# Two PSUM banks for the sums by bucket, one for the second layer's product, in a graph network's message step

## The chip, the cores and the metric

The kernel runs on one core of a Trainium2 chip. The metric is the device time of one execution in microseconds (us). The core's engines run unsynchronized, each through its own instructions in order: TensorE (PE in the profile, its weight loads PEld), VectorE (DVE), ScalarE (ACT), GpSimd (POOL) and SyncE (SP), which issues most of the DMAs. Matmul results land in PSUM, which has eight banks of 2 KB a partition; the kernel uses all eight in its main part.

## The reference, cut to what matters

There are 12,500 nodes with 64 values each and 212,500 edges, sorted by one of their two ends. With h = relu(layernorm(x)):

```python
edge_in = concatenate([h[row], h[col], dist], axis=1)
e = silu(edge_in @ eW1 + eb1)          # first layer of an edge, 129 -> 128
e = silu(e @ eW2 + eb2)                # second layer, 128 -> 128
agg = segment_sum(e, row, num_segments=12500)
out = x + silu(concatenate([h, agg], axis=1) @ nW1 + nb1) @ nW2 + nb2
```

`row` is not the sorted end, so the sum goes to rows that lie in any order.

## The kernel before, in words

Nodes are dealt to NB = 100 buckets of L = 125. A **sending** part goes through the edges in 208 blocks of 1,024 (lines 376 to 517): it forms an edge's part of the first layer that belongs to its sorted end with a matmul (`qp`, line 463), copies it out of PSUM with ScalarE (`qs`, lines 472 and 473) and scatters its rows with indirect DMAs from GpSimd into a table `q` in DRAM, in which each bucket has places of its own. VectorE finds the place of each edge (`oh`, `each`, `mine`, `rank`, `to`; lines 385 to 439) with the help of two matmuls into the bank `counts` (lines 401 and 420).

A **receiving** part takes those rows back, four buckets and 512 edges at a time. `LEVELS` has 18 levels and there are 25 groups of four buckets, so there are 450 steps. Step k goes through these operations (all four tiles of 128 edges together):

- `s_lr` (571): four PE matmuls write `lr`, the edges' places in their bucket, into a bank of the pool `mm` (four banks, shared with `qp`, `pt` and others).
- `s_one_t` (580): DVE compares `lr` with the node numbers, `oneT` (582), and so frees the bank.
- `s_pt` (585): PE transposes the rows and adds the other end's part through `oneT` (591 and 597) into `pt`; ACT's Silu makes `e1` of it (601) and frees the bank.
- `s_bias` (620): ACT copies the second layer's bias `b2f` into a bank `p2` (623).
- `s_p2` (626): PE adds `e1` times `w2` onto it (629); ACT's second Silu makes `e2` (633).
- `s_one` (604): DVE makes `one` (610); the load of a later step's rows is issued here.
- `s_seg` (636): PE sums `e2` by node into the bank `seg` (643).
- `s_add` (645): DVE adds `seg` to `aggT` (654; for the first level it copies, 652). On the last level this also starts `nodes` (272), the node network for the four buckets.

`manual_schedule` fixes the order on PE, DVE, ACT and SP as the program is written. It is the list `turn` that sets it: turn k issues the operations of several steps, and at each `None` (a hook) some of the sending part's pieces.

```python
        turn = [
            (s_pt, 1), (s_add, -2), (s_one_t, 2), None, (s_bias, 1), (s_p2, 0), (s_one, 0), None, (s_seg, -1), None, (s_lr, 3), None,
        ]
```

The number is how far ahead of k the step is. So in turn k the PE runs `pt` of step k + 1, `p2` of k, `seg` of k - 1 and `lr` of k + 3, with `qp` and `counts` matmuls at the hooks. The PSUM pools are opened at lines 302 to 304:

```python
        mm = work.enter_context(tc.tile_pool(name="mm", bufs=4, space=PSUM))
        p2p = work.enter_context(tc.tile_pool(name="p2", bufs=2, space=PSUM))
        sgp = work.enter_context(tc.tile_pool(name="sg", bufs=1, space=PSUM))
```

The pool `sg` holds one bank for `seg` and one for `counts`. With one bank, `seg` of step k - 1 can't begin before `s_add` of step k - 2 has read the bank. With two banks, `s_bias` of k + 1 writes the bank that the second Silu of step k - 1 has read. The loop at 945 to 948 writes each `p2` bank once with a matmul before the first turn.

Of the kernel before, what the change touches and what calls it, by code (L numbers as in the profile page):

```python
# [28 lines left out]
F32 = mybir.dt.float32  # L29
# [6 lines left out]
PSUM = bass.MemoryType.PSUM  # L36
DRAM = bass.MemoryType.DRAM

P = 128
# [12 lines left out]
G = 4  # L52
# [3 lines left out]
LEVELS = [(1, 18, 0), (1, 32, 0), (1, 46, 0)]  # L56
# [18 lines left out]
def tile_gnn(ctx: ExitStack, tc: tile.TileContext, x, src, dst, ew, eW1, eb1, eW2, eb2, nW1, nb1, nW2, nb2, out):  # L75
    nc = tc.nc
    N, D = x.shape
    H = eW2.shape[0]
    E = src.shape[0]
    assert D == 64 and H == P and N % L == 0  # L80
    NB = N // L
# [81 lines left out]
    b2r = const.tile([1, G, H], F32, name="b2r")  # L163
# [15 lines left out]
    ones = const.tile([1, P], F32, name="ones")  # L179
# [92 lines left out]
    def nodes(B, xr, zh, ps, sb, tag):  # L272

        b = B * G

        zs = sb.tile([P, 2, G // 2, L], F32, name="zs", bufs=3)
        z = [ps.tile([P, G // 2, L], F32, name="z", tag=tag) for _ in range(2)]
        for a in range(2):
            nc.tensor.matmul(z[a], w1g, aggT[:, b + a : b + G : 2, :], start=True, stop=True)
        send_out()  # L280
        yield
        for a in range(2):
            nc.vector.tensor_tensor(zs[:, a], z[a], zh[:, a], op=OP.add)
        nc.scalar.activation(zs, zs, AF.Silu, bias=nb1c)
        yield
        o = ps.tile([L, G, D], F32, name="o", tag=tag)
        for t in range(G):
            nc.tensor.matmul(o[:, t, :], zs[:, t % 2, t // 2, :], w2n, start=True, stop=True)
        yield
        os_ = sb.tile([L, G, D], F32, name="os")  # L290
        nc.vector.tensor_tensor(os_, o, xr, op=OP.add)
        unsent.append((out_rows[:, b : b + G, :], os_))
# [7 lines left out]
    top = ctx.enter_context(tc.tile_pool(name="to", bufs=4))  # L300
    with ExitStack() as work:
        mm = work.enter_context(tc.tile_pool(name="mm", bufs=4, space=PSUM))
        p2p = work.enter_context(tc.tile_pool(name="p2", bufs=2, space=PSUM))
        sgp = work.enter_context(tc.tile_pool(name="sg", bufs=1, space=PSUM))
        work.enter_context(
            tc.manual_schedule(
                engines={mybir.EngineType.PE, mybir.EngineType.DVE, mybir.EngineType.Activation, mybir.EngineType.SP}
            )
        )
        full = sgp.tile([P, NB], F32, name="counts")  # L310
        nc.tensor.matmul(full, before, identb[:, :NB], start=True, stop=True)
        nc.vector.memset(full, -1.0)
        mine = cnt.tile(twos, F32, name="mine")
# [209 lines left out]
        steps = [(w, B, n, g) for w, B, n in batches for g in range(n)]  # L523
# [118 lines left out]
            for t, (j, b) in enumerate(tiles):  # L642
                nc.tensor.matmul(item[2][:, b, :], e2[:, t, :], one[:, t, :], start=j < G, stop=j >= G * (n - 1))  # L643

        def s_add(k):
            c, B, n, g = steps[k]
            if g < n - 1:
                return
            v = aggT[:, B * G : B * G + G, :]
            seg = batch.pop((c, B))[2]  # L650
            if c == 0:
                nc.vector.tensor_copy(v, seg)
            else:
                nc.vector.tensor_tensor(v, v, seg, op=OP.add)  # L654
            if c == len(LEVELS) - 1:
                tails.append(nodes(B, *node_in.pop(B), mm, ndp[1], "mm"))
# [2 lines left out]


        turn = [
            (s_pt, 1), (s_add, -2), (s_one_t, 2), None, (s_bias, 1), (s_p2, 0), (s_one, 0), None, (s_seg, -1), None, (s_lr, 3), None,
        ]
        hooks = sum(1 for s in turn if s is None)
        def norm(xs, n, early=False):

            xs = xs[:, :n, :]
            wide = [P, n, D]
            mean = fp.tile([P, NE], F32, name="mean")[:, :n]
            nc.vector.tensor_reduce(mean, xs, AX.X, OP.add)  # L670
            nc.vector.tensor_scalar(mean, mean, 1.0 / D, None, op0=OP.mult)
            cen = fp1.tile([P, NE, D], F32, name="cen")[:, :n]
            nc.vector.tensor_tensor(cen, xs, mean[:, :, None].to_broadcast(wide), op=OP.subtract)
            if early:
                nc.vector.tensor_tensor(xs, cen, cen, op=OP.mult)
            else:
                nc.scalar.activation(xs, cen, AF.Square)
            yield
            var = fp.tile([P, NE], F32, name="var")[:, :n]
            nc.vector.tensor_reduce(var, xs, AX.X, OP.add)  # L680
            nc.vector.tensor_scalar(var, var, 1.0 / D, EPS, op0=OP.mult, op1=OP.add)
            nc.scalar.activation(var, var, AF.Sqrt)
            yield
            nc.vector.reciprocal(var, var)
            nc.vector.scalar_tensor_tensor(xs, cen, 0.0, var[:, :, None].to_broadcast(wide), op0=OP.max, op1=OP.mult)
            yield
# [27 lines left out]
        def normed(b0, n, xs):  # L714
            yield from norm(xs, n)
            yield
            ready.add(b0)
# [158 lines left out]
        with tc.tile_pool(name="lists", bufs=1, side="right") as lp:  # L876
# [23 lines left out]
            nc.sync.dma_start(x0[:, G:, :], x0_rows[:, G:, :])  # L900
            extra_rows(nc.sync.dma_start)
            near, far = norm(x0[:, :G, :], G, True), norm(x0[:, G:, :], NE - G)
            places, table = destinations(), first_rows(0)
            next(near)
# [37 lines left out]
        aggp = ctx.enter_context(tc.tile_pool(name="aggp", bufs=1))  # L942
        aggT = aggp.tile([P, NB, L], F32, name="aggT")
        b2f = aggp.tile([P, G, H], F32, name="b2f")
        for _ in range(2):
            p2 = p2p.tile([P, G, H], F32, name="p2")
            nc.tensor.matmul(p2, ones, b2r, start=True, stop=True)
            nc.scalar.copy(b2f, p2)
        ld2 = work.enter_context(tc.tile_pool(name="ld2", bufs=NQ))
        ndp, lap = [], []  # L950
        pieces = send_all(2 * FIRST, nblocks)
# [13 lines left out]
        for w in range(1, len(LEVELS)):  # L965
            start = w * (NB // G) - NQ
# [2 lines left out]
            marks.append((hooks * (by - first), goal_of(w)))  # L969
        at = 0  # L970
        for k in range(first, len(steps) + 2):
            for s in turn:
                if s is None:
                    while len(marks) > 1 and at >= marks[1][0]:
                        marks.pop(0)
                    if len(marks) > 1:
                        (t0, n0), (t1, n1) = marks[:2]
                        goal = n0 + (n1 - n0) * (at + 1 - t0) / (t1 - t0)
                        while done + 1 <= goal + 0.001:
                            next(pieces, None)  # L980
                            done += 1
                    at += 1
                    for _ in range(2):
                        if not lap and next(feed, 0) == 0:
                            feeding.close()
                            lap.append(keeping.enter_context(tc.tile_pool(name="la", bufs=1, side="right")))
                    if tails:
                        both = tails[at % 2 :: 2][:1] if len(tails) > 1 else tails[:1] * (at % 2)
                        for t in both:
                            if next(t, 0) == 0:  # L990
                                tails.remove(t)
                else:
                    f, ahead = s
                    if 0 <= k + ahead < len(steps):
                        f(k + ahead)
            if k == len(steps) - 8:
                assert done == total
                fp = mm.tile([1, P], F32, name="fp", tag="mm")
                s = cnt.tile([P, 1], F32, name="s")
                nc.vector.tensor_tensor(s, bad[:, 0:1], bad[:, 1:2], op=OP.add)  # L1000
                nc.tensor.transpose(fp, s, ident)
                m = cnt.tile([1, 1], F32, name="m")
                nc.vector.tensor_reduce(m, fp, AX.X, OP.max)
                nc.vector.tensor_copy(flag_i, m)
# [137 lines left out]
```

## Time and profile before

| | |
|---|---|
| median of three runs | 2978.04 us (2963.86 to 2979.62) |
| the profiled execution | 2986.03 us |
| its span, first to last instruction | 2984.2 us |
| sending alone, and the tables | from 0 to about 330 us |
| sending and receiving together | from about 330 to about 2740 us |
| receiving alone, and the node network | from about 2740 us to the end |
| mean granted TensorE clock | 0.877 |

A row of the timeline has the start and the length in us, the engine, the line and the operation, and in brackets how long the engine had been idle and what released it. A row of the waits has the total in us, the number of waits and the longest. A PE row gives the time at which a matmul was taken up; several rows are merged into one with a count.

### The profile page before, as it was taken

To read this page: it belongs to the slowest core of one execution; us is meant where nothing else is said; L and a number is where in the kernel's file an instruction comes from. 1 tells how busy PE (TensorE), PEld (TensorE's weight loads), DVE (VectorE), ACT (ScalarE), POOL (GpSimd) and SP (SyncE) were. 2 spreads that over 40 slices of the span, in tenths; PEclk is the share of its full clock that TensorE was granted. 3 is DMA by queue.
4 is the path that set the end of the run, shared out by engine and by line. 5 is a ranking of instruction groups with operands and counts; after the bars stand their busy time and mean duration, and the time that the engine had idled before them with its cause. 6 is when DMAs were issued, how large, how long until landed. Compare 5 with 4: busy or idle time off the path is not lost.

```text
span 2984.2 us, 49759 instructions
## 1 busy us (share of the span) xinstructions
PE 2368.6 (79%) x17391; PEld 2043.5 (68%) x17391; DVE 1882.5 (63%) x3250; ACT 1165.9 (39%) x3258; POOL 1700.0 (57%) x1712
## 2 busy tenths in 40 slices
PE   2664677778888888888788877888787888888998
PEld 1442566667777777766677766777676777777998
DVE  7553455566666666666666666666666666666755
ACT  2432333334344444433344333344333434344543
POOL 5665656666565655655665566565655656565410
PEclk8555788889998999989899889988988998899999
DMA  4443555444444444444444344443443333333374
GB/s 104 165 156 125 188 181 161 142 141 131 140 139 132 137 136 138 134 128 128 131 140 136 121 131 133 135 135 122 143 143 120 104 106 101 106 104 109 115 225 133
DMA packets 244993, 402.91 MB, mean 135 GB/s; under 512 B 49516, under 2 KB 143647, under 8 KB 244529
## 3 DMA queue, kind: packets, MB, share of 16 engines
q1 hardware_dynamic: 151717, 217.57, 24.7%
q0 software_dynamic: 53536, 123.03, 11.9%
q10 hardware_dynamic: 39482, 59.04, 7.0%
q8 instruction: 139, 2.28, 0.3%
q14 instruction: 119, 0.97, 0.1%
HBM read 192.46 MB, written 207.01 MB: 134 GB/s over the span
## 4 chain that ended last, share of the span: by engine, by line
PE 62%; another core or an unknown queue 15%; issue 8%; ACT 6%; DVE 5%; DMA 2%; SPq 0%; POOL 0%; ACTq 0%; DVEq 0%; POOLq 0%
PE pt L597 13%; PE p L629 12%; PE seg L643 11%; PE qp L463 9%; PE pt L591 7%; PE lr L577 4%; ACT e L601 2%; PE ab L206 2%; DMA qt<-q 1%; ACT qs L472 1%; DVE aggT L654 1%; DVE oneT L582 1%; ACT p L623 1%; PE counts L401 1%
## 5 line engine op out<-in xcount | busy, mean ns | idle before, releaser
L476 POOL DMA_INDIRECT q<-qs,to x1661 | 1669.3, 1005 | 1142.1 <-issue 424.1
L601 ACT ACTIVATE e<-pt 128x512 f32<-128x512 f32 x450 | 269.4, 599 | 1181.4 <-remote 440.7
L654 DVE TENSOR_TENSOR aggT<-aggT,seg 128x500 f32<-128x500 f32 x425 | 285.4, 672 | 496.1 <-remote 133.4
L643 PE MATMUL seg<-one,e 128*128 128x125 f32 x3600 | 528.0, 290 | 79.4 <-DVE aggT L654 46.3
L629 PE MATMUL p<-w,e 128*128 128x128 f32 x3600 | 540.1, 296 | 18.4 <-issue 18.3
L643 PEld LDWEIGHTS seg<-one,e 128*128 128x128 f32 x3600 | 466.6, 201 | 115.8 <-issue 58.6
L629 PEld LDWEIGHTS p<-w,e 128*128 128x128 f32 x3600 | 493.2, 210 | 41.8 <-issue 36.5
L463 PE MATMUL qp<-win,pick 64*128 64x256 f32 x1662 | 386.5, 469 | 110.9 <-ACT e L601 40.2
L582 DVE TENSOR_SCALAR oneT<-lr,part 125x512 f32<-125x512 f32 x450 | 336.0, 747 | 155.4 <-remote 40.0
L472 ACT COPY qs<-qp 128x256 f32<-128x256 f32 x831 | 310.9, 375 | 285.8 <-PE p L629 67.3
L591 PE MATMUL pt<-ident,qt 128*128 128x128 f32 x1800 | 315.7, 303 | 92.3 <-ACT e L601 54.9
L435 DVE TENSOR_TENSOR mine<-oh,counts 128x800 f32<-128x800 bf16 x208 | 204.4, 982 | 221.9 <-PE qp L463 65.3
L633 ACT ACTIVATE e<-p 128x512 f32<-128x512 f32 x450 | 270.0, 600 | 166.4 <-PE p L629 49.2
L463 PEld LDWEIGHTS qp<-win,pick 64*128 64x128 f32 x1662 | 173.5, 205 | 215.0 <-issue 76.4
L577 PE MATMUL lr<-identb,qt 128*125 128x128 bf16 x1800 | 196.7, 231 | 140.7 <-ACT e L601 63.2
L591 PEld LDWEIGHTS pt<-ident,qt 128*128 128x128 f32 x1800 | 213.8, 155 | 133.1 <-ACT e L601 64.3
L610 DVE TENSOR_TENSOR one<-nodes,qt 128x500 f32<-128x500 f32 x450 | 303.4, 674 | 0.0
L597 PE MATMUL pt<-oneT,al 125*128 125x128 f32 x1944 | 300.9, 305 | 3.1 <-issue 2.9
L577 PEld LDWEIGHTS <-qt 128*125 128x125 bf16 x1800 | 167.2, 144 | 178.5 <-issue 149.2
L597 PEld LDWEIGHTS pt<-oneT,al 125*128 125x128 f32 x1944 | 279.1, 220 | 3.6 <-issue 3.5
L623 ACT COPY p<-b2f 128x512 f32<-128x512 f32 x450 | 269.0, 598 | 0.0
L437 DVE TENSOR_REDUCE rank<-mine 128x8 f32<-128x800 f32 x208 | 205.1, 986 | 7.2
(156 smaller groups left out, 1907.5 us busy)
## 6 DMA issues: line engine op xcount, KB each, us to landing
qt<-q SPq DMA_DIRECT2D x450, 288.0 KB
q<-zeros ACTq DMA_DIRECT2D x70, 720.0 KB
q<-qs,to POOLq DMA_INDIRECT x1661
bc<-dests SPq DMA_DIRECT2D x103, 128.0 KB
win<-tb SPq DMA_DIRECT2D x416, 30.0 KB
tb<-got SPq DMA_DIRECT2D x25, 256.0 KB
a_last<-ta SPq DMA_DIRECT2D x25, 256.0 KB
zd<-zn SPq DMA_DIRECT2D x25, 250.0 KB
```

Of the source, the lines that this page charges most:

```text
L463: nc.tensor.matmul(qps[i_][:, :m], pick[half, t * P : (t + 1) * P], win[half, :m], start=True, stop=True)
L472: nc.scalar.copy(qs[:, :m, :H], qp[:, :m, :])
L476: ins = nc.gpsimd.indirect_dma_start(out=q[:], out_offset=bass.IndirectOffsetOnAxis(ap=to[:k, j : j + 1], axis=0), in_=qs[:k, a, :], in_of ...
L577: nc.tensor.matmul(lr[:L, t, :], loc[:, at : at + 1].to_broadcast([P, L]), identb, start=True, stop=True)
L582: nc.vector.tensor_scalar(oneT, st[k].pop("lr")[:L], part1[:L, :], None, op0=OP.is_equal)
L591: nc.tensor.matmul(pt[:, t, :], qt[:, j, :H], ident, is_transpose=True, start=t == 0, stop=False, skip_group_check=True)
L597: nc.tensor.matmul(pt[:, cols, :], a[:L, b, :], oneT[:, cols, :], start=False, stop=True, skip_group_check=True)
L601: nc.scalar.activation(e1, pt, AF.Silu)
L610: nc.vector.tensor_tensor(one.rearrange("p (b j) l -> p b j l", j=n), nodes1[:, None, None, :].to_broadcast(wide), loc[:, tiles[0][1] : ti ...
L629: nc.tensor.matmul(p2[:, t, :], e1[:, t, :], w2, start=False, stop=t == G - 1, skip_group_check=True)
L643: nc.tensor.matmul(item[2][:, b, :], e2[:, t, :], one[:, t, :], start=j < G, stop=j >= G * (n - 1))
L654: nc.vector.tensor_tensor(v, v, seg, op=OP.add)
```

## The change: what it does

- `sg` gets two banks, so `seg` of one step and of the next lie in different ones. `counts` gets a pool of its own, with one bank. `p2` gets one bank instead of two. The sum is eight, as before.
- `s_add` moves from its place after `s_pt` to a place ahead of `s_seg`, for all levels but the last. On the last level it stays where it was.
- `s_bias` of step k + 1 moves from ahead of `s_p2` of step k to behind it, so ACT copies the bias after the second Silu of the step before, into the bank which that Silu has read.
- In the last two turns `s_seg` comes first.
- The loop that writes the `p2` banks once becomes a single pass.

```diff
-        p2p = work.enter_context(tc.tile_pool(name="p2", bufs=2, space=PSUM))
-        sgp = work.enter_context(tc.tile_pool(name="sg", bufs=1, space=PSUM))
+        p2p = work.enter_context(tc.tile_pool(name="p2", bufs=1, space=PSUM))
+        cp = work.enter_context(tc.tile_pool(name="cp", bufs=1, space=PSUM))
+        sgp = work.enter_context(tc.tile_pool(name="sg", bufs=2, space=PSUM))
...
-        full = sgp.tile([P, NB], F32, name="counts")
+        full = cp.tile([P, NB], F32, name="counts")
...
-        def s_add(k):
+        def s_add(k, late=False):
             c, B, n, g = steps[k]
-            if g < n - 1:
+            if g < n - 1 or late != (c < len(LEVELS) - 1):
                 return
...
-            (s_pt, 1), (s_add, -2), (s_one_t, 2), None, (s_bias, 1), (s_p2, 0), (s_one, 0), None, (s_seg, -1), None, (s_lr, 3), None,
+            (s_pt, 1), (s_add, -2), (s_one_t, 2), None, (s_p2, 0), (s_bias, 1), (s_one, 0), None,
+            (lambda k: s_add(k, True), -2), (s_seg, -1), None, (s_lr, 3), None,
         ]
         hooks = sum(1 for s in turn if s is None)
+        ending = [(s_seg, -1)] + [s for s in turn if s is None or s[0] is not s_seg]
...
-        for _ in range(2):
-            p2 = p2p.tile([P, G, H], F32, name="p2")
-            nc.tensor.matmul(p2, ones, b2r, start=True, stop=True)
-            nc.scalar.copy(b2f, p2)
+        p2 = p2p.tile([P, G, H], F32, name="p2")
+        nc.tensor.matmul(p2, ones, b2r, start=True, stop=True)
+        nc.scalar.copy(b2f, p2)
...
-            for s in turn:
+            for s in turn if k < len(steps) else ending:
```

In the built programs the order of the instructions on PE, SP and POOL is the same before and after, but for the matmul of the dropped pass and the last `seg`; only DVE and ACT have another order.

## The prediction

> **What bounds the kernel now.** I read the page first, its busy times, slices and chain:
>
> ```profile
> PE 2368.6 (79%) x17391; PEld 2043.5 (68%) x17391; DVE 1882.5 (63%) x3250; ACT 1165.9 (39%) x3258; POOL 1700.0 (57%) x1712
> ...
> PE   2664677778888888888788877888787888888998
> ...
> PEclk8555788889998999989899889988988998899999
> ...
> PE 62%; another core or an unknown queue 15%; issue 8%; ACT 6%; DVE 5%; DMA 2%; SPq 0%; POOL 0%; ACTq 0%; DVEq 0%; POOLq 0%
> PE pt L597 13%; PE p L629 12%; PE seg L643 11%; PE qp L463 9%; PE pt L591 7%; PE lr L577 4%; ACT e L601 2%; PE ab L206 2%; DMA qt<-q 1%; ACT qs L472 1%; DVE aggT L654 1%; DVE oneT L582 1%; ACT p L623 1%; PE counts L401 1%
> ```
>
> PE is the busiest engine and holds most of the chain; ACT, at 39%, has room. Then the stretches, since sending and receiving overlap only until about 2740 us:
>
> ```profile
> 330.00:2740.00 2410.00, 1974.46 (x14570) 1711.64 (x14569) 1552.25 (x2644) 947.35 (x2666) 1439.49 (x1438) 0.90 0.43 132
> 2740.00:2984.00 244.00, 230.83 (x2022) 222.21 (x2020) 151.44 (x274) 110.28 (x227) 65.39 (x70) 0.98 0.52 155
> ```
>
> The columns are the length, then PE, PEld, DVE, ACT, POOL, the clock and the DMA. After 2740 PE is busy 230.83 of 244 us: little to win. Before, PE idles 2410 - 1974 = 436 us. So the change is decided in that stretch. Its waits, PE's alone (total us, times, longest), and from the view of line 643 those for the addition with weight loads included:
>
> ```profile
> PE lr L577 <- ACT e L601: 63.2, 36, 4.6
> PE pt L591 <- ACT e L601: 54.9, 31, 3.9
> PE seg L643 <- DVE aggT L654: 46.3, 49, 2.6
> ...
> PE qp L463 <- ACT e L601: 40.2, 25, 3.7
> ...
> PE pt L591 <- ACT qs L472: 21.8, 27, 2.7
> ...
> PE lr L577 <- ACT qs L472: 9.2, 7, 2.4
> ...
> PE qp L463 <- ACT qs L472: 8.1, 10, 2.0
> ...
> PE qp L463 <- DVE oneT L582: 5.4, 5, 3.1
> PE lr L577 <- DVE oneT L582: 4.5, 12, 0.8
> ```
>
> ```profile
>   DVE aggT L654: 88.6, 86
> ```
>
> The change goes at the third row: 46.3 us seen by the matmuls, 88.6 us with the loads, which partly see the same wait. The rows on `e` (63.2 + 54.9 + 40.2 = 158 us) are waits for a bank of `mm` and stay.
>
> **One such wait in full.** The timeline, PE, then DVE, then ACT:
>
> ```profile
> 1514.28 0.36 PE L629 MATMUL p<-w,e 128*128 128x128 f32 x1 [0.45 <-issue]
> 1516.45 1.16 PE L643 MATMUL seg<-one,e 128*128 128x125 f32 x8 [1.80 <-DVE aggT L654]
> 1517.45 0.39 PE L577 MATMUL lr<-identb,qt 128*125 128x128 bf16 x4
> ...
> 1518.46 0.62 PE L591 MATMUL pt<-ident,qt 128*128 128x128 f32 x4
> ```
>
> ```profile
> 1515.72 0.68 DVE L654 TENSOR_TENSOR aggT<-aggT,seg 128x500 f32<-128x500 f32 x1 [2.08 <-PE p L629]
> 1516.32 0.74 DVE L582 TENSOR_SCALAR oneT<-lr,part 125x512 f32<-125x512 f32 x1
> ```
>
> ```profile
> 1516.21 0.60 ACT L601 ACTIVATE e<-pt 128x512 f32<-128x512 f32 x1
> 1516.70 0.60 ACT L623 COPY p<-b2f 128x512 f32<-128x512 f32 x1
> 1517.21 0.60 ACT L633 ACTIVATE e<-p 128x512 f32<-128x512 f32 x1
> 1517.70 0.38 ACT L472 COPY qs<-qp 128x256 f32<-128x256 f32 x1
> ```
>
> ACT and DVE both stand still until about 1515.7 and then run off at once what they owe: PE's results reach them in a bunch. These bunches set the rhythm of the stretch; the change doesn't remove them. It changes only how far PE may run ahead until the next bunch, and what it waits for behind it.
>
> **The change part by part.** The sum is made against the profiled execution, 2986.03 us; the runs shown have their median at 2978.04, 8.0 lower, so I take 8.0 off at the end.
>
> *Two banks for `seg`, and the later addition.* `seg` then needs the addition of two steps before, long done. In the example it could go at 1514.64 instead of 1516.45, 1.81 us sooner. What is late next: `lr`, at 1517.45, wants its bank from `oneT`, which stands behind the addition. With that gone from ahead of it `oneT` ends about 0.6 sooner, at 1516.46, so `lr` gains about 0.9. Next `pt`, at 1518.46, wants a bank that the `qs` copy of 1517.70 (ends 1518.08) frees, and gains only 0.3. So of a wait between a sixth and a half is kept: of 88.6 us 15 to 44; the ends are nothing kept and all of it. I take 0.4, nearer the half because several of the waits have `lr`, not `pt`, next: **-35 us** (0 to -88.6).
>
> *`oneT` ahead of the addition.* PE's rows on `oneT`: 5.4 in 5 waits and 4.5 in 12. At most an addition's 0.68 goes from each: 5 x 0.68 + 4.5 = 7.9. I take **-7** (0 to -9.9). VectorE's own time is the same. The late addition waits for a `seg` of the turn before, so it holds up nothing that stands behind it (the hooks' `mine`, `rank` and `to`, on which POOL waits).
>
> *One bank for `p2`.* Now `p2` of step k + 1 waits for the bias copy, that for the second Silu of k, and that for `p2` of k. Before, the copy was done ahead of the Silu. A Silu and a copy take 0.60 + 0.60, with about 0.05 to hand over, so `p2` may start 1.25 us after the Silu's start. Where ACT was late anyway (1516.70, 1517.21) Silu and copy only change places. Where ACT waited for `p2` itself it bites; in the trace of before 18 turns have a Silu that waited and a next `p2` less than 1.25 us behind its start, the first and the last of them being
>
> ```profile
> 529.16 0.60 ACT L633 ACTIVATE e<-p 128x512 f32<-128x512 f32 x1 [1.54 <-PE pt L591]
> ```
>
> ```profile
> 529.84 2.09 PE L629 MATMUL p<-w,e 128*128 128x128 f32 x8
> ```
>
> ```profile
> 2618.92 0.60 ACT L633 ACTIVATE e<-p 128x512 f32<-128x512 f32 x1 [2.19 <-PE pt L597]
> ```
>
> ```profile
> 2618.36 0.39 PE L629 MATMUL p<-w,e 128*128 128x128 f32 x2
> ...
> 2620.33 0.38 PE L629 MATMUL p<-w,e 128*128 128x128 f32 x2 [0.82 <-issue]
> 2622.61 1.13 PE L643 MATMUL seg<-one,e 128*128 128x125 f32 x8 [1.90 <-DVE aggT L654]
> ```
>
> The first lacks 529.16 + 1.25 - 529.84 = 0.57 us, the last 2618.92 + 1.25 - 2618.36 = 1.81; the 18 together 26.3. The last also shows why not all of it is lost: `p2` would start at 2620.17, take 0.9, and `seg` could follow at 2621.1, still ahead of its 2622.61, as it no longer waits for the addition. I take half, **+13 us** (0 to 26.3).
>
> *The bias copy behind the Silu.* ACT's total is the same, but where the Silu had to wait, the copy filled that wait before; now it stands ahead of what follows, mostly the `qs` copies, which free banks for PE and feed POOL. The group of the second Silu in the stretch, and its idle time:
>
> ```profile
> L633 ACT ACTIVATE e<-p 128x512 f32<-128x512 f32 x397 | 238.4, 601 | 147.4 <-PE p L629 30.6 <-remote 26.7 <-PE qp L463 21.3
> ```
>
> It idles 147.4 us ahead of the 397. The copy also has to wait for the Silu's end, where before the Silu began 0.51 us after a copy of 0.60 (1516.70, 1517.21): some 0.1 us a turn, in ACT's spare time. PE waited for `qs` 27 + 7 + 10 = 44 times; were each of them 0.65 later, it would be 29 us. Only those behind a Silu that waited are, I take a third: **+9 us** (0 to 29).
>
> *The rest.* The dropped pass of `p2` lies at 140 us, ahead of any turn; its two matmul passes are 2 x 1.06 us. In that slice of 75 us, the second in the page, PE is busy six tenths, so the idle rest covers it and I cost it at nothing; at -2 if not covered:
>
> ```profile
> L947 PE MATMUL p<-b2r,ones x4: 1056/1056/1215, 140.0 to 142.7; 1*128 1x512 f32 x4
> ```
>
> The last turns gain at most one `seg`, under 1.2 us: nothing. No DMA moves, and SP's and POOL's orders stay.
>
> The sum: -35 - 7 + 13 + 9 = -20 us. 2986.03 - 20 = 2966; less 8.0 that is **2958 us** as a median, 0.7% below 2978.04.
>
> **A rule of the Trainium skill.** "TensorE: Matmul & The Clock Gate", section "HAM oscillation — how this bites in real kernels", says of one kernel that "Adding PSUM double-buffering gave no further gain". That speaks against the first term; by it the gain would be 0, and it bears on the third rival. Here the row of 46.3 us shows a real wait for the bank, but also three times as much for other banks, so the trace neither refutes nor confirms it.
>
> **The rivals.**
>
> - *The second layer's bank takes the wait over (slower).* The one-bank loop isn't gone, it moves from `seg` to `p2`: a bunch that comes late now stops PE one product sooner, and its way back is longer: Silu and copy, 1.25 us, instead of an addition, 0.68 + 0.05. If all 49 of PE's waits come back so, nothing is won, 49 x (1.25 - 0.73) = 25 us are lost, and the two ACT terms make it more: 25 + 9 = 34, less 7 for `oneT`: 2978 + 27 = **3005 us**. It decides from the point where PE is less than 1.25 us behind the Silu's start in more than about 49 turns; in the trace of before it is 18, which speaks against it. For it speaks that PE will run further ahead there.
> - *All of the wait goes, and ACT's terms stay hidden.* 46.3 + 9.9 = 56 us: 2978 - 56 = **2922 us**. Against it: `lr` and `pt` in the example.
> - *The next bank takes it over (no change).* `e`'s 158 us are bank waits of `mm` at `lr`, `pt` and `qp`, PE's next instructions. If they grow by what `seg` loses, -35 becomes about -15 (the sixth) and the sum is -15 - 7 + 13 + 9 = 0: **2978 us**.
> - *It doesn't do what it says.* `seg` still waits for DVE, for `one`; were DVE late with the addition by a whole turn, the wait would stay. DVE, busy 1552 of 2410 us, is not: this belongs to the no-change case.
>
> **How the numbers follow.** The forecast has 0.36, all of it gone 0.12, no change 0.27, taken over by `p2` 0.25. What a measurement of this kernel can tell from no change is about 0.5%, 15 us. The forecast lies 20 us below with neighbours on both sides of that line; a sliver of 0.02 of it I give to the no-change side, and as much of no change to faster. So faster 0.48, same 0.27, slower 0.25. The range: from 2915, where the matmuls' 46.3 and the loads' part of `oneT` go and ACT costs nothing (2978 - 56, and 7 for a third of a hundredth more clock: 1974 x 0.0033 / 0.90), to 3005, the slower rival. Cases of both signs are likely, so beside it the forecast's own range, from its first term alone (44 to 15 us): 2949 to 2978.
>
> **What would show it.** In the stretch to 2740: `seg`'s wait for `aggT` should be nearly gone (under 5 us from 46.3), the step that I am surest of. PE's waits for `e` should grow by 10 to 25 us. A new row, PE `p` waiting for ACT `p`, should stand at 10 to 20 us; at 40 or more the slower rival is right. PE's waits for `qs` should go from 39 to about 48. PE's idle time in the stretch should fall by some 20 us, and the stretch after 2740 stay within 2 us. Wrong would I be if the bunches themselves change, since everything else is measured against them, or if the clock leaves 0.90.

## The result, and the profile after

The changed kernel is slower: 2998.43 us as a median of 16 runs (2984.72 to 3013.08), against 2970.32 for the kernel before in 16 runs (2955.02 to 2985.0). The ratio is 1.0093, with a 95% interval of 1.0078 to 1.0109. The forecast was 2958: 20 us to the good, where 28 were lost. The profiled execution took 3004.4 us (span 3002.6), at a mean clock of 0.876.

The page of the changed kernel: busy times, slices of PE and its clock, and the chain. Line numbers are one higher than before.

```profile
PE 2377.1 (79%) x17389; PEld 2052.5 (68%) x17389; DVE 1874.2 (62%) x3250; ACT 1228.1 (41%) x3257; POOL 1701.2 (57%) x1712
...
PE   2664776778888888888778887888777888888998
...
PEclk9655788888898899988988989899888888899999
...
PE 62%; another core or an unknown queue 13%; issue 9%; ACT 7%; DVE 5%; DMA 2%; POOL 0%; SPq 0%; ACTq 0%; DVEq 0%; POOLq 0%
PE p L630 13%; PE pt L598 13%; PE seg L644 11%; PE qp L464 8%; PE pt L592 8%; PE lr L578 4%; ACT e L634 2%; ACT e L602 2%; PE ab L206 2%; ACT qs L473 2%; DMA qt<-q 1%; DVE oneT L583 1%; PE counts L402 1%; PE z L279 1%
```

The addition (`aggT`) and the bias copy (`p`) are no longer among the chain's lines; the second Silu (`e` L634) has come in, and `qs` has gone from 1% to 2%. ACT is busy 62 us longer, though it does one instruction less. The stretches, with the columns as before:

```profile
330.00:2740.00 2410.00, 1960.96 (x14456) 1703.83 (x14452) 1529.62 (x2622) 993.38 (x2647) 1430.03 (x1429) 0.89 0.43 131
2740.00:2984.00 244.00, 235.19 (x2059) 226.69 (x2057) 157.73 (x283) 123.39 (x239) 76.29 (x80) 0.98 0.53 160
```

In the same 2410 us PE takes up 14,456 matmuls instead of 14,570, 0.8% fewer: the loss lies in the sending and receiving stretch. PE idles 2410 - 1961 = 449 us there, from 436. PE's waits in that stretch:

```profile
PE pt L592 <- ACT e L602: 56.2, 37, 4.2
PE pt L592 <- ACT qs L473: 55.4, 35, 3.8
PE lr L578 <- ACT e L602: 49.0, 25, 4.3
...
PE qp L464 <- ACT e L602: 43.9, 21, 6.4
...
PE qp L464 <- DVE oneT L583: 20.9, 13, 5.2
PE qp L464 <- ACT qs L473: 18.2, 15, 3.2
...
PE p L630 <- ACT p L624: 11.6, 15, 1.8
...
PE p L630 <- ACT e L634: 8.3, 5, 2.8
```

There is no row for `seg` waiting on `aggT` any more; it was 46.3 us. In its place the rows on `qs`, with one more of 2.8 us at `lr`, make 76.4 us, from 39.1, and `p2` waits 19.9 us for ACT where it waited for no engine. The waits for `e` didn't grow: 149.1 from 158.3. On ACT, the second Silu in that stretch:

```profile
L634 ACT ACTIVATE e<-p 128x512 f32<-128x512 f32 x394 | 236.0, 599 | 265.7 <-PE p L630 84.1 <-remote 47.5 <-PE pt L598 29.3
```

ACT idles 265.7 us ahead of it instead of 147.4. What filled that time before, the bias copy, now runs behind the Silu.

The loss can be read from GpSimd too. Its scatters in the page of before and in that of the changed kernel:

```profile
L476 POOL DMA_INDIRECT q<-qs,to x1661 | 1669.3, 1005 | 1142.1 <-issue 424.1
```

```profile
L477 POOL DMA_INDIRECT q<-qs,to x1661 | 1669.8, 1005 | 1159.3 <-issue 424.9
```

They take as long as before, and GpSimd idles 17.2 us longer ahead of them, where the span has grown by 18.4. In the stretch its waits for `qs` go from 533.4 to 555.5 us. The last scatter ends at 2829 us before and 2846 after, so sending doesn't end at 2740 as the table ahead of the prediction has it; and in all twenty traces of this case the program ends 156 to 158 us after its last scatter. What is lost or gained shows in when that one comes.

### The profile page after: what moved, and what is told of

Read it like the earlier page. It is cut to its first block, busy times and chain, and to the rows that moved or that the text cites. A ratio compares the mean times of both kernels' runs of the same rounds, so it can differ in the third digit from the quotient of the medians.

```text
span 3002.6 us, 50305 instructions
## 1 busy us (share of the span) xinstructions
PE 2377.1 (79%) x17389; PEld 2052.5 (68%) x17389; DVE 1874.2 (62%) x3250; ACT 1228.1 (41%) x3257; POOL 1701.2 (57%) x1712
## 4 chain that ended last, share of the span: by engine, by line
PE 62%; another core or an unknown queue 13%; issue 9%; ACT 7%; DVE 5%; DMA 2%; POOL 0%; SPq 0%; ACTq 0%; DVEq 0%; POOLq 0%
PE p L630 13%; PE pt L598 13%; PE seg L644 11%; PE qp L464 8%; PE pt L592 8%; PE lr L578 4%; ACT e L634 2%; ACT e L602 2%; PE ab L206 2%; ACT qs L473 2%; DMA qt<-q 1%; DVE oneT L583 1%; PE counts L402 1%; PE z L279 1%
## 5 line engine op out<-in xcount | busy, mean ns | idle before, releaser
L630 PE MATMUL p<-w,e 128*128 128x128 f32 x3600 | 552.1, 302 | 24.7 <-ACT p L624 11.6
L630 PEld LDWEIGHTS p<-w,e 128*128 128x128 f32 x3600 | 502.0, 215 | 52.9 <-issue 20.9
L644 PEld LDWEIGHTS seg<-one,e 128*128 128x128 f32 x3600 | 473.2, 203 | 53.2 <-issue 45.7
L634 ACT ACTIVATE e<-p 128x512 f32<-128x512 f32 x450 | 269.4, 599 | 310.6 <-PE p L630 122.4
L598 PE MATMUL pt<-oneT,al 125*128 125x128 f32 x1944 | 292.1, 299 | 2.3 <-issue 2.3
L598 PEld LDWEIGHTS pt<-oneT,al 125*128 125x128 f32 x1944 | 270.1, 214 | 2.3 <-issue 2.2
L624 ACT COPY p<-b2f 128x512 f32<-128x512 f32 x450 | 265.4, 590 | 14.1
L598 PE MATMUL pt<-oneT,ae 125*128 125x128 f32 x1360 | 212.4, 303 | 9.5 <-issue 9.0
```

The costliest lines, as they stand in the source:

```text
L598: nc.tensor.matmul(pt[:, cols, :], a[:L, b, :], oneT[:, cols, :], start=False, stop=True, skip_group_check=True)
L630: nc.tensor.matmul(p2[:, t, :], e1[:, t, :], w2, start=False, stop=t == G - 1, skip_group_check=True)
L634: nc.scalar.activation(e2, p2, AF.Silu)
```

## The experiments

**Theories.** *A:* ScalarE's order costs the time. The bias copy now stands between the second Silu and the `qs` copies, which free PE's banks and feed GpSimd. *B:* the single `p2` bank costs it: PE's product must wait for the Silu and the copy. *C:* the later addition holds VectorE up.

**Two kinds of batches.** Each batch ran the kernel before beside its own kernels, on one chip. In three of the five batches before took 2399, 2399 and 2404 us, at a mean granted clock of 0.948 to 0.949; in two it took 2925 and 2969 us, like the 2970 of the result, at 0.883 and 0.879. So there are two sets of results, which I call the 2400 and the 2950 runs. That the chip makes the difference isn't shown: the record gives the same chip number for one of the batches at 2399 us and for the one at 2969. Times are compared only within a batch, ratios only within a set.

GpSimd differs as well. Its row in the changed kernel's page in a 2400 run (experiment 5):

```profile
L477 POOL DMA_INDIRECT q<-qs,to x1661 | 1676.4, 1009 | 538.0 <-issue 305.5
```

It idles 538 us ahead of its scatters instead of 1159. From 330 us on, 5 of its pauses are longer than 0.35 us, 8 us in all, against 310 pauses and 672 us in the changed kernel's trace at 3003 us. So in the 2400 runs GpSimd goes from one scatter to the next with little more than a steady 0.3 us between them, and what PE and ACT wait for has little room to cost or save time.

All ratios, with their 95% intervals:

| kernel | 2950 runs | 2400 runs |
|---|---|---|
| the changed kernel | 1.0093 [1.0078, 1.0109], 1.0074 [1.0045, 1.0102], 1.0118 [1.0085, 1.0152] | 0.9963 [0.9950, 0.9976] |
| before, copy behind the Silu | 1.0053 [1.0028, 1.0079] | 1.0019 [1.0005, 1.0034] |
| the same, one `p2` bank | 1.0093 [1.0062, 1.0123] | 1.0015 [1.0004, 1.0026] |
| changed, early addition | not measured | 1.0004 [0.9994, 1.0014], 1.0013 [0.9999, 1.0027] |
| changed, copy at the end of the turn | 1.0016 [0.9989, 1.0042] | 0.9964 [0.9952, 0.9975] |
| changed, copy in the middle | 0.9981 [0.9956, 1.0006] | 0.9973 [0.9959, 0.9987] |
| before, copy in the middle | not measured | 1.0002 [0.9990, 1.0015] |
| before, no copy | 0.9943 [0.9921, 0.9965] | 1.0001 [0.9986, 1.0015] |
| changed, no copy | 0.9938 [0.9914, 0.9962] | 0.9982 [0.9967, 0.9997] |

Where I give the difference of two medians of one batch, the interval in brackets is from resampling their runs.

**1. The bias copy behind the Silu, nothing else.** In before's `turn`:

```diff
-None, (s_bias, 1), (s_p2, 0), (s_one, 0), None,
+None, (s_p2, 0), (s_bias, 1), (s_one, 0), None,
```

> The kernel before with one edit: the bias copy stands behind the second Silu; two p2 banks and one seg bank stay, and the addition stays early. Theory A (ScalarE's order: the copy now stands ahead of the qs copies, which free banks for the PE): 15 to 35 us slower than before, and the PE's waits for the qs copies between 330 and 2740 us rise from 39.1 to 65 us or more. Theory B (the single p2 bank makes the PE wait for Silu and copy): within 6 us of before, since with two banks the bank that the copy takes has long been read; qs waits at 39 to 45. Theory C (the late addition holds VectorE up): within 6 us of before.

> Before, with only the bias copy of the next step put behind the second Silu; two p2 banks, one seg bank, early addition. On a chip that takes 2970 us theory A (the copy stands ahead of the qs copies) asks for 15 to 30 us more than before and for PE's waits on qs to go from 39 to over 65 us; theory B for no difference over 5 us, since p2 keeps two banks; the seg wait on aggT stays at 40 us or more in both. On a chip that takes 2400 us the earlier look gave 1.0019, and it should come again within 0.002.

In the 2400 run it costs 4 us (2403.43 against 2399.35). In the 2950 run it costs 15.7 us [9, 22], within A's 15 to 30. But PE's waits on `qs` are at 43.1 us there, not over 65 (before wasn't traced in that batch), and a new one is nearly as large, though `p2` still has two banks:

```profile
PE pt L591 <- ACT qs L472: 31.4, 27, 4.4
PE p L629 <- ACT p L623: 31.0, 19, 3.1
```

So the order alone makes the product wait: the copy for the next step can't begin before a Silu that itself waits for PE. B expected no difference from this kernel; A expected another row. `seg` waits 33.9 us for `aggT`, where 40 or more was expected.

**2. The same, and `p2` with one bank.**

```diff
-        p2p = work.enter_context(tc.tile_pool(name="p2", bufs=2, space=PSUM))
+        p2p = work.enter_context(tc.tile_pool(name="p2", bufs=1, space=PSUM))
```

> The kernel before with the copy behind the Silu and one p2 bank; one seg bank, and the addition early. Theory A: within 8 us of the run with two banks and the copy behind, so 15 to 35 us slower than before. Theory B: 30 to 60 us slower than before (the changed kernel's 28 us and what two seg banks give back), with the PE waiting 20 us or more for the bias copy or the second Silu. Theory C: within 6 us of before.

> The same as the run with the copy behind the Silu, and p2 with one bank. Its difference to that run is the price of the single bank alone. Theory B: 10 us or more on a chip that takes 2970 us, with a wait of p2 on the copy and the Silu of 15 us or more in PE; theory A: under 5 us, the loss being there already with two banks. On a chip that takes 2400 us the earlier look had 1.0015 against 1.0019: nothing.

In the 2950 run the loss of the second `p2` bank costs 18.4 us [4, 24] more; in the 2400 run nothing (-1.5 [-6, 4]). B asked for 10 us or more, and has it; A asked for under 5. But B's reason doesn't show: `p2` waits 16.0 + 11.9 = 27.9 us, less than the 31.0 with two banks, while the waits on `qs` go from 43.1 to 68.3. What the bank does to ACT shows in the timeline. With two banks (the kernel of experiment 1), ACT:

```profile
1002.72 0.60 ACT L633 ACTIVATE e<-p 128x512 f32<-128x512 f32 x1 [0.36 <-PE p L629]
1003.22 0.59 ACT L623 COPY p<-b2f 128x512 f32<-128x512 f32 x1
1003.73 0.38 ACT L472 COPY qs<-qp 128x256 f32<-128x256 f32 x1
```

With one bank (the changed kernel), ACT, and then PE:

```profile
1529.89 0.60 ACT L634 ACTIVATE e<-p 128x512 f32<-128x512 f32 x1 [0.97 <-PE lr L578]
1530.52 0.59 ACT L624 COPY p<-b2f 128x512 f32<-128x512 f32 x1
1531.04 0.37 ACT L473 COPY qs<-qp 128x256 f32<-128x256 f32 x1
```

```profile
1529.24 0.70 PE L464 MATMUL qp<-win,pick 64*128 64x256 f32 x4
1531.46 0.66 PE L592 MATMUL pt<-ident,qt 128*128 128x128 f32 x4 [1.51 <-ACT e L634]
```

With two banks the copy begins 0.50 us after the Silu's start, ahead of its end; with one it begins 0.63 after it, behind its end, since it writes the bank that the Silu reads (0.49 and 0.63 us are the medians of the 449 such pairs in each of the two traces). So `qs` begins 1.15 us after the Silu's start instead of 1.01; in the copy's own place it could begin at 0.50. In the last fence PE takes up `pt` at 1531.46, 0.05 us after the `qs` copy's end at 1531.41. (The row names the Silu, but that had ended at 1530.49.) With the copy out of the way that could be 0.65 us sooner.

**3. The changed kernel with the addition at its early place.**

```diff
-            if g < n - 1 or late != (c < len(LEVELS) - 1):
+            if g < n - 1 or late:
```

> The changed kernel with the addition early on every level, as before. Theories A and B: within 6 us of the changed kernel, so 22 to 34 us slower than before. Theory C: 10 to 25 us faster than the changed kernel, and the PE's waits for oneT fall from 29.5 us between 330 and 2740 us to about 10.

> The changed kernel with the addition back at its early place on all levels. Against the changed kernel (1.0074 on a chip where before takes 2925 us, 1.0093 where it takes 2970 us) it is the price of the move alone. Theory C (the late addition holds VectorE up): 5 us or more faster than the changed kernel, 1.003 to 1.006, and PE's waits on oneT fall. My own forecast: slower than the changed kernel by 3 to 8 us, 1.009 to 1.011, since oneT stands behind the addition again. On a chip that takes 2400 us it gave 1.0004 before.

Both batches were 2400 ones: 1.0004 and 1.0013, where the changed kernel has 0.9963. The early addition is the slower place there, by some 10 us, the other way round from C. For the 2950 runs, where the loss is, it stays untried; but experiments 7 and 8 keep the later addition and lose nothing there, so C can't be the main cause.

**4. The changed kernel with the copy at the end of the turn,** behind the `qs` copies of all the turn's hooks:

```diff
-(s_p2, 0), (s_bias, 1), (s_one, 0), None,
+(s_p2, 0), (s_one, 0), None,
...
-(s_seg, -1), None, (s_lr, 3), None,
+(s_seg, -1), None, (s_lr, 3), None, (s_bias, 1),
```

> The changed kernel with the bias copy at the end of a turn, behind the last hook, where ScalarE next waits for pt. One p2 bank, two seg banks and the late addition stay. Theory A: 20 to 40 us faster than the changed kernel, so from 12 us faster than before to 8 slower; the PE's waits for the qs copies fall from 76 us to 35 to 50. Theory B: no faster than the changed kernel, as the copy comes later still and p2 waits for it at least as long (20 us or more). Theory C: within 6 us of the changed kernel.

> The changed kernel with the bias copy put at the very end of the turn, behind the qs copies of all hooks. Theory A: on a chip that takes 2970 us the loss of 28 us goes, PE's waits on qs fall from 76 to under 50 us and the time is at or below before's (0.985 to 1.002). Theory B: p2 waits longer still, as the copy comes later, over 40 us, and the time is 1.01 or more. On a chip that takes 2400 us 0.996 should come again within 0.002.

In the 2950 run it takes 17.7 us [12, 26] from the changed kernel's loss. PE's waits in it:

```profile
PE p L630 <- ACT p L624: 75.9, 49, 4.3
...
PE pt L592 <- ACT qs L473: 24.2, 19, 3.0
```

The waits on `qs` are 31.0 us in all, from 58.0 in the changed kernel of the same batch. `p2` waits for the copy 75.9 us, from 30.7, and the kernel is still faster. This is against B as the main cause, and says that a long row of PE's waits needn't cost its length.

For A speaks that in this batch the waits on `qs` stand in the order of the times. PE's and GpSimd's up to 2740 us are 31 and 486 us here (2932.54 us as a median), 43 and 509 in experiment 1 (2940.60), 58 and 524 in the changed kernel (2950.18), 68 and 543 in experiment 2 (2958.97). It is one trace of each.

**5. The changed kernel again,** without an edit, in three batches.

> The changed kernel itself, unedited, beside the kernel before on whatever chip this falls on. The kernel before took 2970 us on the chip of the result and 2399 us on the chip of the first experiments. If the loss comes from the edits themselves (theories A, ScalarE's copy ahead of the qs copies, and B, PE waiting for Silu and copy in the one p2 bank), the ratio is above 1.004 on either chip. If it needs the late bunches of the chip that takes 2970 us, it is 1.008 to 1.011 there and within 0.3% of 1 on a chip that takes 2400 us. The early addition gave 1.0004 on the quick chip; theory C (the late addition holds VectorE up) asks for more than 1.002 here on such a chip.

> The changed kernel itself. Where before takes 2925 to 2970 us: 1.006 to 1.010, as measured twice. Where before takes 2400 us it hasn't been timed: its relatives there gave 1.0004 and 1.0013 with the addition early, 0.9964 with the copy at the end of the turn and 0.9973 in the middle, so if the copy's place matters there too, 0.999 to 1.002; if only the early addition had cost something, 0.996.

> The changed kernel itself again. Where before takes 2925 to 2970 us: 1.007 to 1.012, as measured three times. Where before takes 2400 us, for the first time: 0.996 to 0.999, since the copy in the middle gave 0.9973, at the end of the turn 0.9964, and PE hardly waits for ScalarE there, so the copy's place should matter little; 1.000 or more would say that it matters there too.

In the 2950 runs it loses 25 and 34 us. In the 2400 run it gains 7.9 us [6, 14]: 2395.91 against 2403.83. The same program is slower on the one and faster on the other. So the edits alone don't decide the sign.

**6. Before without the bias copies,** so that the output lacks the second layer's bias:

```diff
-            nc.scalar.copy(p2, b2f)
...
-                    p2[:, t, :], e1[:, t, :], w2, start=False, stop=t == G - 1, skip_group_check=True
+                    p2[:, t, :], e1[:, t, :], w2, start=True, stop=True, skip_group_check=True
```

> Before, with the copies of the second layer's bias left out (the product starts the bank itself), so the output lacks that bias; banks and places as in before. 450 copies of 0.60 us go from ScalarE, which before did in its idle time or ahead of the second Silu. Theory A (what counts is what stands ahead of the qs copies on ScalarE): a gain of 15 us or more, with PE's waits on qs below 25 us from 39. Theory B (what counts is how long one turn of Silu and copy holds p2, and ScalarE's load doesn't matter): within 10 us of before, 0.997 to 1.003.

> Before, without the copies of the second layer's bias, so the output lacks that bias. Where before takes 2925 to 2970 us, theory A (what counts is what stands ahead of the qs copies on ScalarE) asks for a gain of 15 us or more and PE's waits on qs below 25 us; theory B (the loop through p2 counts, ScalarE's load doesn't) for 0.997 to 1.003. Where before takes 2400 us: 1.000 again, within 0.0015.

**7. The changed kernel without them,** by the same edit.

> The changed kernel without the bias copies, so the output lacks that bias too. p2 has one bank and must still wait for the second Silu of the step before, but not for a copy. Theory A: the loss goes with the copy, and the two seg banks show their gain; the time is below that of the run without the copy and with before's banks by some 10 us (two copies of the same chain, 0.3%). Theory B: the one bank alone still costs; p2's waits on the Silu stay above 20 us and the time is above that of the run without the copy and with before's banks.

> The changed kernel without the bias copies (the output lacks that bias): one p2 bank, two seg banks, late addition. Where before takes 2925 to 2970 us, theory A: 0.990 to 0.997, below the run without the copies on before's banks, since the loss went with the copy. Theory B: 1.002 or more, with waits of p2 on the second Silu of 20 us or more, since the one bank still makes the product wait. Where before takes 2400 us: 0.998 again, within 0.0015.

In the 2400 runs the copies are worth nothing to before (2399.09 against 2399.16). In the 2950 runs before gains 16.5 us [9, 27] without them and the changed kernel 51.5 us [42, 63]: 2952.24 and 2950.80 us are left, -1.4 us [-9, 4] apart. So all of the loss hangs on the copy, and one `p2` bank without a copy costs no more than two `seg` banks with the later addition bring. B in its plain form falls: it asked for 20 us of waits of `p2` on the Silu, and there are 8.0. A has the gain that it asked for, but not its row: PE still waits 35.6 us for `qs` in before without the copies, not under 25. The stretch to 2740 us in before without the copies, PE's waits and the stretch itself:

```profile
PE lr L577 <- ACT e L601: 64.3, 31, 5.5
PE pt L591 <- ACT e L601: 61.6, 39, 4.0
PE seg L642 <- DVE aggT L653: 60.9, 49, 3.4
PE qp L463 <- ACT e L601: 36.5, 21, 6.1
...
PE seg L642 <- issue: 21.1, 39, 2.3
```

```profile
330.00:2740.00 2410.00, 1995.82 (x14841) 1737.19 (x14841) 1573.99 (x2680) 771.10 (x2300) 1459.22 (x1454) 0.90 0.45 133
```

And in the changed kernel without them:

```profile
PE pt L592 <- ACT e L602: 75.0, 42, 4.8
PE qp L464 <- ACT e L602: 44.1, 24, 5.3
PE seg L643 <- issue: 42.0, 75, 1.2
...
PE lr L578 <- ACT e L602: 36.5, 23, 4.6
...
PE counts L421 <- DVE counts L419: 17.6, 8, 4.2
```

```profile
330.00:2740.00 2410.00, 2007.47 (x14886) 1744.74 (x14883) 1565.54 (x2683) 772.79 (x2305) 1460.28 (x1456) 0.90 0.45 134
```

60.9 us of waiting for `aggT` are gone, and the matmuls done are 45 more of 14,841, 0.3%. Most of the wait has moved, as PE's idle time in the stretch falls by only 11.7 us: for `e` it is 162.4 and 155.6, with `pt` taking what `lr` had; `counts` waits 17.6 instead of 8.1, and `seg` 42.0 instead of 21.1 with nothing shown to wait for.

**8. The changed kernel with the copy in the middle of the turn,** behind the second hook, so behind the `qs` copies that come right after the Silu:

```diff
-(s_p2, 0), (s_bias, 1), (s_one, 0), None,
+(s_p2, 0), (s_one, 0), None, (s_bias, 1),
```

> The changed kernel with the copy behind the second hook, so behind that hook's qs copies and ahead of the later ones: a place between the changed kernel's (1.0074 on a chip where before takes 2925 us) and that at the end of the turn (1.0016). Theory A: between the two, 1.002 to 1.006, with PE's waits on qs between 31 and 58 us. Theory B: p2's waits between 40 us (changed) and 78 us (end of the turn), and the time above the changed kernel's, since the copy comes later for the product.

> The changed kernel with the copy behind the second hook. Where before takes 2925 to 2970 us: theory A, between the changed kernel and the one with the copy at the end of the turn, 1.002 to 1.006; theory B, above the changed kernel, 1.008 or more. Where before takes 2400 us: 0.9973 again, within 0.0015.

In the 2950 run it is 37.4 us [26, 52] faster than the changed kernel: all of the loss is gone, more than A's graded forecast of 1.002 to 1.006, and the opposite of B's. PE waits for `qs` 40.1 us, from 61.1 in the changed kernel of that batch, and for the copy not much longer (19.9 from 14.1). PE's waits on `qs` stand in the order of the times in this batch too: 32, 36, 40 and 61 us for 2951 and 2952 (experiments 7 and 6), 2965 and 3002; GpSimd's, 516, 518, 515 and 537, only set the last apart. In the 2400 run it is 0.9973. It is the best version with the whole output that came out: level with before or a little ahead in both kinds, though in the 2950 run the interval holds 1.

One rival is left from the edits: they also bring semaphore instructions. ACT has 450 of 17 ns ahead of the second Silu in every kernel with the copy moved, where before has 2; but before without the copies has 448 and is the faster. PE has 256 of 51 ns ahead of the product with one bank in experiment 2, and none in experiment 1; but experiments 4 and 8 have 422 and 337 and lose little or nothing. So they aren't the main price.

**9. Before with the copy in the middle,** on the old banks, by the same move in before's `turn`.

> Before with only the bias copy of the next step moved behind the second hook, ahead of seg: two p2 banks, one seg bank, early addition. Where before takes 2925 to 2970 us: the changed banks with the copy at this place gave 0.9981. If the two seg banks and the later addition bring nothing net, as the pair without copies says, this gives the same, 0.995 to 1.001, with seg's wait for aggT at 30 us or more; if they bring 9 us or more, this is slower, above 1.001. Where before takes 2400 us (0.9973 with the changed banks, 1.0019 with the copy directly behind the Silu on the old banks): 1.000 to 1.002, with seg's wait still near 97 us, if it's the banks that help there.

It fell on a 2400 run: 1.0002. The changed kernel of that batch is 9.3 us [6, 15] faster, so what is gained there doesn't come from the copy's place. Nor do the banks alone bring it: with them and the early addition (experiment 3) there was no gain. PE's waits up to 2200 us, while sending still runs there, in before with the copy in the middle:

```profile
PE seg L643 <- DVE aggT L654: 97.3, 73, 4.1
PE lr L577 <- DMA qt<-q: 42.7, 43, 4.3
```

and in the changed kernel:

```profile
PE lr L578 <- DMA qt<-q: 58.3, 58, 3.0
PE qp L464 <- DVE oneT L583: 22.7, 23, 2.8
PE pt L592 <- DVE oneT L583: 19.8, 22, 4.0
PE seg L644 <- DVE aggT L655: 18.4, 14, 2.8
```

There too most of the wait moves: 97.3 to 18.4 on `aggT`, but `qt` and `oneT` take it over. And what is gained shows elsewhere. GpSimd idles 539.5 us ahead of its scatters in the one trace and 538.0 in the other, but the scatters take 1690.2 us, 1018 ns each, in the first and 1676.4 us, 1009 ns each, in the second: 13.8 of the 15.3 us between the two spans. In the ten traces of 2400 runs this time goes from 1676 to 1690 us as the span goes from 2388 to 2403. Why the scatters are shorter, no run shows.

## Why the prediction was wrong, step by step

*Two `seg` banks and the later addition, -35, and `oneT` ahead of the addition, -7.* This is the step that failed. I took PE's wait at `seg` as time on the path and asked only how much of it the next two banks would take back in one example. The wait was also too large from the start: 88.6 adds the matmuls' 46.3 us and the weight loads' 42.3, and laid over each other they cover 57.3 us; 0.4 of that is 23, not 35. Measured without the copies, both terms together with the one bank are -1.4 us [-9, 4]; with them, the changed kernel against the one-bank kernel of experiment 2, -8.8 us [-15, 6], where the forecast had -42. The row itself did go, 46.3 to none, as I was surest of. PE's waits on `oneT` didn't fall but rose, 9.9 to 29.5 us with those of 6.5 at `pt` and 2.1 at `lr`. My third rival, the next bank takes it over, had this term right, though not on `e`, whose rows fell. Of the rule that I quoted from the Trainium skill, "TensorE: Matmul & The Clock Gate", section "HAM oscillation — how this bites in real kernels", that a second PSUM buffer gave no further gain there, this pair is another case in the 2950 run; what the changed kernel gained in the 2400 run, 0.4%, came with shorter scatters (experiment 9).

*One bank for `p2`, +13.* It measured +18.4 [4, 24], near enough in size, but not for my reason. I reckoned what PE lacks behind a late Silu. The waits of `p2` came as forecast (10 to 20; 19.9), yet they came with two banks too, from the order alone. By the two timelines and the waits on `qs`, the bank's own price lies on ACT, where copy and Silu don't overlap; no run sets this apart. It is 0.13 us a turn, which I had named as "some 0.1 us a turn" and put at nothing, "in ACT's spare time". Without a copy its price wasn't measured alone; together with the first two terms it came to the -1.4 us above.

*The bias copy behind the Silu, +9.* It measured +15.7 [9, 22]: the right direction, somewhat small. The delay of `qs` that I took, 0.65 us, is the one that the timeline shows with one bank; with two it is 0.51. Whether the 15.7 us come by PE's waits on `qs`, as I had it, isn't shown: with the order alone these were 43.1 us, and the product's wait for the copy, which I had put down to the one bank, was 31.0. In the changed kernel the waits on `qs` went from 39.1 us to 76.4 (58 and 61 in its two other profiles), where I had 48: a third of 44 waits was too small a share. The Silu stands idle longer than in the trace of before, 265.7 us instead of 147.4, as the copy no longer fills the gap, and all of that time now comes ahead of the `qs` copies with the copy still to do.

The terms as measured with the copy in its place, in the batch where before takes 2925 us: 15.7 + 18.4 - 8.8 = 25.3, and the changed kernel there is 2950.18 - 2924.86 = 25.3 us slower. (The steps add up by construction; the intervals reach 5 to 15 us to a side.) Against the forecast's -7 - 35, +13 and +9, some 33 of the 45 us that it was off lie in the terms of `seg` and `oneT`.

*The rest.* After the product of step 400, which begins at 2751 us before and 2767 after, 233 and 236 us remain: nearly as forecast, little happens there. The clock of the stretch reads 0.90 and 0.89, and a move from 0.90 was to be a sign of being wrong; but PE is busy 135.5 and 135.7 ns there for each matmul, so the clock makes only some 2 us. Over whole runs the mean clock was a little lower in the slower kernel, 0.876 from 0.883 in one batch and 0.870 from 0.879 in the other; whether as a cause or as a consequence of the waiting stays open.

*The rivals.* The slower one had 3005 us, and 2998 came, but by its own sign, a `p2` row of 40 us or more, it isn't what happened: that row has 19.9. The kernel with the copy at the end has 75.9 and is faster. It counted 25 us for `p2`'s way back and 9 for ACT's order; of the two it is ACT's part that the runs bear out.

*The bunches.* I said that they set the rhythm and that the change doesn't remove them. The first Silu's idle time shows them, in the changed kernel of the batch where before takes 2969 us and, up to 2200 us, in that where it takes 2404:

```profile
L602 ACT ACTIVATE e<-pt 128x512 f32<-128x512 f32 x393 | 235.0, 598 | 955.6 <-remote 364.7 <-PE qp L464 201.1 <-PE pt L598 93.5
```

```profile
L602 ACT ACTIVATE e<-pt 128x512 f32<-128x512 f32 x402 | 240.2, 597 | 560.7 <-PE pt L598 506.3 <-PE counts L421 50.2 <-PE pt L592 4.2
```

In the first, most of the idle time ends at something other than the product it needs; in the second, 506.3 of 560.7 us end with just that product. There PE hardly waits for ACT at all (`qs`: 1.5 us in all up to 2200), and GpSimd has hardly a pause to lengthen, so the copy's place costs little. That the bunches are what makes ACT's order dear is my reading of the two sets; no run took them away with all else alike. Why they come in some batches and not in others stays open.

## What to carry to other kernels

A wait that a view names isn't a gain until the next three waits behind it have been priced: here 46 to 97 us of waiting for one bank were worth 0 to 10 us. Ask also which engine's last instruction the end follows: here it always came 156 to 158 us after GpSimd's last scatter, although PE was the busiest engine. When work on an in-order engine moves from ahead of an instruction that waits to behind it, price all that queues behind it there, and see whether a shared bank also ends the overlap of the two. Put a filler behind the urgent instructions, not between them: the same copy, one hook later, took back the whole loss in the 2950 run.

## What the runs showed of the hardware

- The same program took about 2400 us in some batches, at a mean granted clock near 0.95, and 2925 to 2970 us in others, near 0.88, and one change had opposite signs there (0.9963 and 1.0074 to 1.0118). In the 2950 runs ACT sees products late: in the changed kernel's trace at 3001 us, 69 of the 272 second Silus that waited began over 0.3 us after the record of their product ended, 224 us together; in the one at 2388 us it was 2 of 363, 0.8 us.
- ScalarE started a copy 0.49 us after the start of a 0.60 us Silu where it wrote another bank, and 0.63 us after it where it wrote the bank that the Silu reads (medians of 449 pairs each). Over the kernel this made ACT busy 1230 us instead of 1183 (experiments 2 and 1).
- Taking 450 copies of 0.60 us from ScalarE, which is busy 39% of the span, gained before 16.5 us in the 2950 run and 0 in the 2400 run, where GpSimd's scatters left hardly a gap. "Perfetto Trace Analysis" of the Trainium skill, section "Optimizing Tensor Performance", advises letting matmul groups rotate through PSUM banks so that their reading overlaps the next group's matmuls. Here a second bank for `p2` was worth 18.4 us, by the timelines through the overlap of two instructions on ScalarE, and one for `seg` little.
